# Four graph-attention layers on one core: normed rows turned by DMA instead of TensorE, and pieces of layer 0 moved from VectorE to ScalarE and GpSimd

## The chip, the cores and the metric

The kernel runs on one core of a Trainium2 chip. The core has TensorE (PE, matrix products, with a weight load of its own, PEld), VectorE (DVE), ScalarE (ACT), GpSimd (POOL), a queue engine (SP) that mostly starts transfers, and 16 DMA engines. The metric is the device time of one execution in microseconds (us); smaller is better. The kernel before takes 3050.61 us, the median of three runs between 3050.41 and 3050.61.

## The reference

x holds 16 graphs (batches) of 1024 nodes with 256 features, in float32; one adjacency matrix of 1024 x 1024 is shared by all. Four layers follow each other, each of the form

```
h = max(layernorm(x), 0)
x = x + attention_layer(h, adj)
```

- Layers 0 and 3 are graph attention with 4 heads of 64 features: Wh = h W; the score of the pair (i, j) is leaky_relu(s_i + t_j) with s and t from two vectors; softmax over the neighbours j; a weighted sum of Wh; ELU.
- Layer 1 is the same with one head of 256 features.
- Layer 2 takes its scores from a product of two projections, leaky_relu((h W1)(h W2)^T), masks and normalizes them in the same way, multiplies h W3, and ends in a ReLU.

All 16 batches are independent of each other; within one batch each layer needs the one before, and each needs all 1024 rows of x.

## The kernel before, in words

The kernel is written out for all 16 batches and 4 layers by `fast` (a second path, `general`, is there for inputs with extreme values and isn't entered here). A batch's x is one tile of 128 partitions x 8 row tiles x 256 features; 5 such tiles are held at a time, so several batches are at different layers at once.

**The order.** `Plan` is a planner in the kernel's source. Every piece of work is a step with an engine, a cost in us, a due time, the steps it must follow, and the buffers that it takes and gives. `Plan.order` plays this forward, on each engine always the due step whose inputs and buffers are there, and the instructions are then emitted in that order. So the order on each engine is fixed when the kernel is built, and each engine works through its own list. `PERIOD`, `START`, `LEAD`, `STEP`, `WHEN`, `LATER` and `AHEAD` set the due times: batch b starts layer l at about (b + START[l]) periods. A transfer is planned by `landed` as 256 KB in about 0.8 us and then 2.2 us until it is seen.

**One layer of one batch.** `Layer.prologue` takes mean and variance (L813, L814: on DVE), gets 1/sqrt on POOL (L849) and a shift on DVE (L852). Then, for four pairs of row tiles:

1. ACT norms two row tiles into `h` (L886, two instructions of 128x256).
2. TensorE turns them, so that features lie on partitions (`turned`, `turn`, L585). It treats a float32 value as two 16-bit halves, and turns each half with a 16-bit identity: 16 matmuls of 64x128 for a pair. This keeps every bit.
3. ACT joins the halves again from PSUM into `hTp` or `hT` (`kept`, L918, 128x1024 of 16 bits).
4. TensorE multiplies with the weights (`projected`, L572). ACT takes exponentials of the score columns (L949, L952), and the values are scaled by one of them: with one head on ACT (L954), with four heads on DVE (`scaled`, L960).

The score rows go to DRAM and come back spread over all partitions (`er_d`, `row`: L1028, L1041 on SP). In layers 0 and 3 (`steps_a`) DVE then builds one weight tile p of 128x512 per head, half and key tile (`weigh`, L1089: the larger of row and key factor, times the mask), and TensorE multiplies it with the values into `acc` (`attend`). After 8 key tiles the sum is inverted (L1122) and divided: on DVE (L1133), or on ACT, four instructions (L1136), where `filling` holds, which is layer 0 of batches 0 to 2 and layer 3 of batches 14 and 15. `elu` makes the ELU on ACT and DVE (L1060, L1061, L1065) and adds it to x on DVE (L1066). Layers 1 and 2 (`steps_b`) build p for all 8 key tiles of a half (L1179 in layer 1; L1206, L1207, L1211, L1212 in layer 2) and then multiply a query tile at a time into `accb`.

The first prologue of the run and the last (`direct`) differ: their score rows are spread by TensorE (L1002) and not by DRAM.

The mask is made once: the adjacency is compared with 0, turned by TensorE, and kept as four tiles of 16-bit floats.

Buffers that matter here: 8 p tiles, 4 PSUM tiles `pp` for all short products, 2 `acc` and 2 `accb`, 4 `h`, 2 `hTp`, 3 rows for four heads.

Of the kernel before, what the change touches and what calls it, by code (L numbers as in the profile page):

```python
# [10 lines left out]
BF16 = mybir.dt.bfloat16  # L11
I32 = mybir.dt.int32
U16 = mybir.dt.uint16
AF = mybir.ActivationFunctionType
OP = mybir.AluOpType
# [4 lines left out]
P = 128  # L20
# [20 lines left out]

PERIOD, EARLY = 190.0, 0.76
START = {0: 0.0, 1: 1.12, 2: 2.28, 3: 3.57}
LEAD = {0: 0.55, 1: 0.69, 2: 0.43, 3: 1.98}
STEP = {0: 0.0278, 1: 0.0451, 2: 0.105, 3: 0.0624}
WHEN = {  # L50
    (1, "weights"): ((-0.2631, 0.0266), (-0.1849, 0.0202)),
    (1, "attended"): ((0.3063, 0.0435), (0.1514, 0.2476)),
    (2, "weights"): ((0.0671, 0.0134), (0.1481, 0.0064)),
    (2, "attended"): ((0.514, 0.0835), (0.5175, 0.0062)),
}

LATER = {
    (0, 1): -0.958, (0, 2): -0.007, (1, 0): 0.06, (1, 1): 0.8, (2, 0): -0.065, (2, 2): 0.245, (3, 0): -0.357,
    (13, 3): 0.24, (15, 2): 0.02,
}  # L60
AHEAD = {
    (0, 2): 0.54, (1, 0): 0.48, (1, 1): 0.26, (2, 0): 0.16, (3, 0): -0.1,
}
# [466 lines left out]
def fast(  # L530
# [22 lines left out]
    bufs = {  # L553
        "x": 5, "val4": 2, "val1": 2, "hq": 1, "row4": 3, "row1": 2, "h": 4, "hTp": 2, "p": 8, "p1": 18,
        "u": 2, "o": 1, "ex4": 1, "o1": 2, "ex1": 2, "pp": 4, "acc": 2, "accb": 2,
# [44 lines left out]

    mask = [[const.tile([P, HT, HALF], BF16, name=f"mask{i}{j}") for j in range(2)] for i in range(2)]
    rdens = const.tile([P, B, NT], F32, name="rdens")
# [15 lines left out]
    def load_x(b, due, after=()):  # L618

        res = []  # L620
        for k in range(2):

            def fn(k=k):
                if k == 0:
                    x_tiles[b] = buf("x", [P, NT, F], name="xt")
                its = slice(k * HT, (k + 1) * HT)
                nc.sync.dma_start(
                    out=x_tiles[b][:, its, :], in_=x[b].rearrange("(t p) f -> p t f", p=P)[:, its, :]
                )

            s = plan.add(SP, 0.5, due, fn, after, take=() if k else ("x",))
            after = (s,)
            res += [landed(s, due, 512)] * HT
        return res
# [184 lines left out]
    class Layer:  # L819
        def __init__(self, b, layer):  # L820
            self.b, self.layer = b, layer
            self.heads, self.gat = LAYERS[layer]
            self.closed = []

            self.filling = layer == 0 and b < 3 or layer == 3 and b >= B - 2

        def prologue(self, due, step, stats, direct=False):
# [10 lines left out]
            ready = []  # L838
            parts = (slice(0, HT), slice(HT, NT)) if direct else (slice(0, NT),)
            for n, its in enumerate(parts):  # L840

# [27 lines left out]

                at = due - 2 * (direct and n == 0)  # L870
                s = plan.add(DVE, 0.2, at, norm, (*stats[its], ready[-1] if n else None))
# [3 lines left out]
            copies, evicted = [], []  # L875
            turns = {}
            run = 2
            for t0 in range(0, NT, run):
                at = due + t0 // 2 * step
                pairs, norms = range(t0, t0 + run, 2), []  # L880
                for t1 in pairs:

                    def normed(t0=t1):
                        for t in (t0, t0 + 1):
                            h = T["h", t] = buf("h", [P, F])
                            nc.scalar.activation(  # L886
                                h,
                                x_tiles[b][:, t, :],
                                AF.Relu,
                                bias=T["shift"][:, t : t + 1],  # L890
                                scale=T["rstd"][:, t : t + 1],
                            )

                    take = () if norms else ("h",) * run
                    norms.append(plan.add(ACT, 1.2, at, normed, (ready[t1], *norms), take=take))

                def turned(pairs=pairs):
                    for t0 in pairs:
                        tp = T["tp", t0] = buf("pp", [P, 2, KC, 2 * P], BF16)
                        for k in range(2):  # L900
                            bits = halves(T["h", t0 + k])
                            for c in range(KC):
                                for side in range(2):
                                    turn(tp[:, side, c, k * P : (k + 1) * P], bits[:, side, c * P : (c + 1) * P])

                n = len(pairs)
                s = plan.add(PE, 0.47 * n, at, turned, norms, take=("pp",) * n, give=("h", "h") * n)
                turns.update(dict.fromkeys(pairs, s))
            for n, t0 in enumerate(range(0, NT, 2)):
                at, s = due + n * step, turns[t0]  # L910

                def kept(t0=t0):
                    if self.gat:
                        T["hT", t0] = buf("hTp", [P, KC, 2 * P])
                    else:
                        T["hT", t0] = self.hT[:, :, t0 * P : (t0 + 2) * P]
                    bits = T["hT", t0].bitcast(U16).rearrange("p c (q s) -> p c q s", s=2)
                    nc.scalar.copy(bits, T["tp", t0].bitcast(U16).rearrange("p s c q -> p c q s"))  # L918

                s = plan.add(ACT, 0.95, at, kept, (s,), take=("hTp",) if self.gat else (), give=("pp",))  # L920
                copies.append(s)
                for k in range(2):
# [17 lines left out]

                    def evict(t=t):
                        to = self.val[:, t, :, :d]
                        of = T["pv", t][:, :F].rearrange("p (h d) -> p h d", h=heads)
                        if not self.gat:
                            nc.scalar.copy(to, of)
                            return
                        a = self.val[:, t, :, d : d + 1]

                        nc.scalar.activation(  # L949
                            a, T["pv", t][:, F + heads : cols].unsqueeze(2), AF.Exp, scale=1.0 / (SLOPE - 1.0)  # L950
                        )
                        nc.scalar.activation(self.ke[:, :, t], T["pv", t][:, F:cols], AF.Exp)  # L952
                        if heads == 1:
                            nc.scalar.mul(to, of, a[:, 0, :])  # L954

# [5 lines left out]

                    many = heads > 1
                    cost = 0.4 if many or not self.gat else 0.8
                    s2 = plan.add(ACT, cost, at, evict, (s2,), give=() if many else ("pp",))
# [85 lines left out]
        def elu(self, T, key, its, due, after, sizes, cols, give):  # L1050

            tag = f"ex{sizes[0]}"
            first, last = cols[0] == 0, cols[1] == F
            xs = lambda: x_tiles[self.b][:, its[0] : its[1], cols[0] : cols[1]]

            def up():
                if first:
                    T["ex", key] = buf(tag, [P, its[1] - its[0], F])
                o, ex = T["o", key][:, :, cols[0] : cols[1]], T["ex", key][:, :, cols[0] : cols[1]]
                nc.scalar.activation(ex, o, AF.Exp)  # L1060
                nc.scalar.activation(ex, ex, AF.Relu, bias=1.0, scale=-1.0)  # L1061

            def down():
                o, ex = T["o", key][:, :, cols[0] : cols[1]], T["ex", key][:, :, cols[0] : cols[1]]
                nc.vector.scalar_tensor_tensor(o, ex, -1.0, o, op0=OP.mult, op1=OP.max)  # L1065
                nc.vector.tensor_add(xs(), xs(), o)  # L1066

            s = plan.add(ACT, sizes[1], due, up, after, take=(tag,) if first else ())
            s = plan.add(DVE, sizes[2], due, down, (s,), give=(tag, *give) if last else give)
            if last:  # L1070
                for t in range(its[0], its[1]):
                    self.finish(t, due, (s,))
            return s
# [4 lines left out]
    def steps_a(lay, due, span):  # L1078
# [4 lines left out]
        for i in range(n):  # L1083
# [43 lines left out]
            def divide(half=half, hd=hd, on_act=on_act):  # L1127
# [11 lines left out]
            s = plan.add(  # L1139
                *((ACT, 0.8) if on_act else (DVE, 0.44)), at - early[0], divide, (s,),  # L1140
                take=("o",) if hd == 0 else (), give=("acc",),
            )

            if ending:
# [218 lines left out]
    for start, b, layer in sorted(order):  # L1363
# [8 lines left out]
        else:  # L1372
            due, step = SOON, 0.1
            stats = [statistics(b, t, due - (3 if t < HT else 1), (loads[b][t],)) for t in range(NT)]
        lay.prologue(due, step, stats, direct=(b, layer) in ((0, 0), (B - 1, 3)))
# [70 lines left out]
```

## Time and profile before

| | us |
|---|---|
| median of 3 runs | 3050.61 |
| the profiled execution, its own time | 3051.08 |
| its span, first to last instruction | 3049.3 |
| TensorE busy | 3009.3 (99%) |
| DVE busy | 2719.1 (89%) |
| ACT busy | 1461.6 (48%) |
| POOL busy | 127.6 (4%) |
| one batch in the middle (954.99 to 1140.39) | 185.40 |

The profile is one execution, taken by the hardware profiler. A row of its groups reads: source line, engine, operation, output <- inputs, shapes, count | busy time of the group in us, mean ns of one | idle time of the engine just before, and what ended it. Busy time counts overlapping neighbours once, so busy over count is less than the mean. "Waits" name who waited for whom. The chain is the work that ended last, followed back to the start. Matmul ends are modelled, so a busy TensorE isn't one at its peak. Lines such as L572 and L585 are those of helpers that every product or turn goes through. Transfers are issued by SP in the order of its list; its waits are listed apart.

### The profile page before, as it was taken

The numbers are of one execution on the slowest core, as the hardware profiler recorded it, in microseconds if no ns is written. First come the engines' busy times: TensorE is split into PE (matmuls) and PEld (weight loads), VectorE is DVE, ScalarE is ACT, GpSimd is POOL, SyncE is SP. The second block draws the span as 40 slices with busy tenths as digits, with TensorE's granted clock in tenths as the row PEclk, the third lists the DMA queues.
The fourth block names the chain that finished last, engine by engine and source line by source line (L and its number), as shares of the span: only waits on it lengthen the run. The fifth ranks groups of instructions, "written<-read, shape, count | busy, mean of one in ns | idle before, by whom it ended". The sixth has DMA issues, their size and how long they took to land.

```text
span 3049.3 us, 115063 instructions
## 1 busy us (share of the span) xinstructions
PE 3009.3 (99%) x52018; PEld 2508.5 (82%) x52018; DVE 2719.1 (89%) x5551; ACT 1461.6 (48%) x3352; POOL 127.6 (4%) x115
## 2 busy tenths in 40 slices
PE   7999999999999999999999999999999999999998
PEld 6887978778797887978888797887978879786877
DVE  8999968989889898998989989898998989986788
ACT  5563556544544446344454543546344463444443
POOL 1000000000000000000000000000000000000000
PEclk9999999999999999999999999999999999999999
DMA  3110003111010111101111011110111101000110
GB/s 127 51 51 23 27 16 97 38 40 48 20 58 26 37 55 25 58 21 37 51 34 55 19 41 47 37 48 18 52 37 37 55 21 46 23 30 25 30 33 24
DMA packets 82161, 123.41 MB, mean 40 GB/s; under 512 B 6976, under 2 KB 42496, under 8 KB 81664
## 3 DMA queue, kind: packets, MB, share of 16 engines
q1 hardware_dynamic: 81248, 115.47, 12.6%
q8 instruction: 409, 6.70, 0.9%
q14 instruction: 88, 0.72, 0.1%
q10 hardware_dynamic: 416, 0.52, 0.1%
HBM read 98.63 MB, written 17.33 MB: 38 GB/s over the span
## 4 chain that ended last, share of the span: by engine, by line
PE 95%; DVE 4%; issue 0%; DMA 0%; ACT 0%; SPq 0%; DVEq 0%
PE pp L572 33%; PE acc L572 30%; PE accb L572 29%; PE pp L585 4%; DVE p L1089 2%; DVE bn L813 0%; DVE xt L1066 0%; DMA xt<-in_x_dram 0%; DVE o L1065 0%; DVE mv L814 0%; PE pp L1002 0%; PE tpm L585 0%; PE er L585 0%; DVE rden L1122 0%; DVE parts L1308 0%
## 5 line engine op out<-in xcount | busy, mean ns | idle before, releaser
L1089 DVE SCALAR_TENSOR_TENSOR p<-row,ke,mask 128x512 f32<-128x512 f32 x2048 | 1413.2, 744 | 57.9 <-PE acc L572 54.4
L572 PEld LDWEIGHTS acc<-val,p 128*64 128x64 f32 x32768 | 1078.5, 139 | 71.5 <-issue 37.0
L572 PE MATMUL acc<-val,p 128*64 128x65 f32 x32768 | 1087.9, 223 | 17.6 <-DVE p L1089 16.9
L572 PE MATMUL accb<-val,p 128*64 128x257 f32 x8192 | 929.2, 380 | 0.4 <-issue 0.4
L572 PEld LDWEIGHTS accb<-val,p 128*64 128x64 f32 x8192 | 766.6, 136 | 103.2 <-issue 7.0
L572 PE MATMUL pp<-qT,hT 128*64 128x512 f32 x2048 | 457.6, 592 | 0.0
L572 PE MATMUL pp<-w,hTp 128*64 128x264 f32 (+1 forms) x3072 | 378.8, 386 | 0.0
L572 PEld LDWEIGHTS pp<-qT,hT 128*64 128x64 f32 x2048 | 189.1, 137 | 206.5 <-issue 204.3
L572 PEld LDWEIGHTS pp<-w,hTp 128*64 128x64 f32 x3072 | 267.6, 137 | 53.9 <-issue 7.7
L1246 ACT ACTIVATE o<-accb,rdens 128x256 f32<-128x256 f32 x128 | 60.6, 474 | 471.1 <-DVE rdens L1238 433.0
L886 ACT ACTIVATE h<-xt,nshift,rstd 128x256 f32<-128x256 f32 x512 | 273.1, 596 | 12.9 <-DVE nshift L852 12.9
L1211 DVE SCALAR_TENSOR_TENSOR p<-u,p 128x512 f32<-128x512 f32 x256 | 175.8, 687 | 62.1 <-ACT p L1207 61.5
L1206 ACT ACTIVATE u<-pp 128x512 f32<-128x512 f32 x256 | 152.7, 596 | 152.6 <-PE pp L572 137.3
L813 DVE BATCH_NORM_STATS2 bn<-xt 128x6 f32<-128x256 f32 x512 | 212.4, 415 | 14.8 <-DMA xt<-in_x_dram 5.2
L1244 ACT ACTIVATE o<-accb,rden 128x256 f32<-128x256 f32 x128 | 60.4, 472 | 337.9 <-DVE rden L1238 337.9
L918 ACT COPY hTp<-pp 128x1024 uint16<-128x1024 uint16 x192 | 190.4, 1011 | 58.2 <-PE pp L585 56.9
L849 POOL TENSOR_TENSOR rstd<-rstd,neg_half 128x8 f32<-128x8 f32 (+1 forms) x66 | 117.9, 1786 | 2108.0 <-DVE rstd L846 1643.8
L1212 DVE TENSOR_TENSOR p<-p,mask 128x512 f32<-128x512 f32 x256 | 177.2, 692 | 8.8
L1179 DVE SCALAR_TENSOR_TENSOR p<-row,ke,mask 128x512 f32<-128x512 f32 x256 | 183.6, 741 | 0.0
L1207 ACT ACTIVATE p<-pp,shift_col 128x512 f32<-128x512 f32 x256 | 174.8, 683 | 0.0
L585 PEld LDWEIGHTS <-h 128*64 128x64 bf16 x4096 | 149.4, 111 | 21.3 <-issue 13.4
L1060 ACT ACTIVATE ex<-o 128x1024 f32<-128x1024 f32 (+1 forms) x195 | 122.1, 626 | 90.6 <-DVE o L1133 86.3
(84 smaller groups left out, 1910.9 us busy)
## 6 DMA issues: line engine op xcount, KB each, us to landing
row<-er_d SPq DMA_DIRECT2D x272, 256.0 KB
xt<-in_x_dram SPq DMA_DIRECT2D x32, 512.0 KB
out_dram<-xt SPq DMA_DIRECT2D x31, 512.0 KB
raw<-in_adj_dram SPq DMA_DIRECT2D x4, 1024.0 KB
raw<-in_adj_dram SPq DMA_DIRECT2D x16, 256.0 KB
w<-in_L_gnn_W_dram SPq DMA_DIRECT2D x2, 256.0 KB
wraw<-in_L_gnn_W_dram SPq DMA_DIRECT2D x2, 256.0 KB
er_d<-er_s SPq DMA_DIRECT2D x30, 16.0 KB
```

Source lines behind the costliest of these rows:

```text
L572: nc.tensor.matmul(to[c : c + COLS], stationary[:, c : c + COLS], moving, start=start, stop=stop, skip_group_check=True,)
L585: nc.tensor.transpose(to[c : c + COLS], of[:, c : c + COLS], ident_b)
L813: nc.vector.bn_stats(st, x_tiles[b][:, t, :])
L886: nc.scalar.activation(h, x_tiles[b][:, t, :], AF.Relu, bias=T["shift"][:, t : t + 1], scale=T["rstd"][:, t : t + 1],)
L918: nc.scalar.copy(bits, T["tp", t0].bitcast(U16).rearrange("p s c q -> p c q s"))
L1060: nc.scalar.activation(ex, o, AF.Exp)
L1089: nc.vector.scalar_tensor_tensor(p, lay.rows[half, hd], lay.ke[:, lay.heads + hd, jt : jt + 1], mask_of(half, jt), op0=OP.max, op1=OP.mult)
L1179: nc.vector.scalar_tensor_tensor(p, lay.rows[half, 0], lay.ke[:, 1, jt : jt + 1], mask_of(half, jt), op0=OP.max, op1=OP.mult)
L1206: nc.scalar.activation(u, e, AF.Exp, scale=1.0 - SLOPE)
L1207: nc.scalar.activation(p, e, AF.Exp, bias=shift_col, scale=SLOPE)
L1211: nc.vector.scalar_tensor_tensor(p, u, 1.0, p, op0=OP.max, op1=OP.mult)
L1212: nc.vector.tensor_mul(p, p, mask_of(half, jt))
```

## The change

The turning of normed rows leaves TensorE in 62 of 64 prologues. ACT splits each normed pair into planes of 16-bit halves (`split`), SP starts a DMA that transposes 8 blocks of 128x128 (`move`), and ACT joins the halves from the landed tile (`kept`). The two `direct` prologues turn float32 whole on TensorE, 4 transposes a pair, and copy. `filling` now holds for layer 0 of every batch, and where it holds (and the prologue isn't direct) ACT also scales the values, four instructions a tile, in place of DVE; ACT divides in all of layer 0; and POOL adds the ELU to x. The mask is 8-bit; with two tiles `planes` and two `turned` more, the on-chip memory it gives up is used. The first batch's x comes in three parts (2, 2 and 4 row tiles) rather than two. All due times are set anew. The product lists carry 4096 fewer 16-bit transposes of h and 32 float32 ones more; SP carries 248 transposing transfers more, POOL 35 additions.

```diff
+PARTS = (((0, 4), (4, 8)), ((0, 2), (2, 4), (4, 8)))
-PERIOD, EARLY = 190.0, 0.76
-START = {0: 0.0, 1: 1.12, 2: 2.28, 3: 3.57}
-LEAD = {0: 0.55, 1: 0.69, 2: 0.43, 3: 1.98}
-STEP = {0: 0.0278, 1: 0.0451, 2: 0.105, 3: 0.0624}
+PERIOD, EARLY = 190.0, 0.74
+START = {0: 0.0, 1: 0.96, 2: 2.3, 3: 3.63}
+LEAD = {0: 0.7841, 1: 0.4991, 2: 0.193, 3: 1.8815}
+STEP = {0: 0.028, 1: 0.0997, 2: 0.0747, 3: 0.0167}
...
-        "x": 5, "val4": 2, "val1": 2, "hq": 1, "row4": 3, "row1": 2, "h": 4, "hTp": 2, "p": 8, "p1": 18,
+        "x": 5, "val4": 2, "val1": 2, "hq": 1, "row4": 3, "row1": 2, "h": 4, "planes": 2, "turned": 2, "hTp": 2, "p": 8, "p1": 18,
...
-    mask = [[const.tile([P, HT, HALF], BF16, name=f"mask{i}{j}") for j in range(2)] for i in range(2)]
+    mask = [[const.tile([P, HT, HALF], U8, name=f"mask{i}{j}") for j in range(2)] for i in range(2)]
...
-        for k in range(2):
+        for t0, t1 in PARTS[b == 0]:
...
-            self.filling = layer == 0 and b < 3 or layer == 3 and b >= B - 2
+            self.filling = layer == 0 or layer == 3 and b >= B - 2
...
-                def turned(pairs=pairs):
-                    for t0 in pairs:
-                        tp = T["tp", t0] = buf("pp", [P, 2, KC, 2 * P], BF16)
-                        for k in range(2):
-                            bits = halves(T["h", t0 + k])
-                            for c in range(KC):
-                                for side in range(2):
-                                    turn(tp[:, side, c, k * P : (k + 1) * P], bits[:, side, c * P : (c + 1) * P])
...
+                def turned(t0=t0):
+                    tp = T["tp", t0] = buf("pp", [P, KC, 2 * P])
+                    for k in range(2):
+                        for c in range(KC):
+                            nc.tensor.transpose(
+                                tp[:, c, k * P : (k + 1) * P], T["h", t0 + k][:, c * P : (c + 1) * P], ident
                             )
...
+                def split(t0=t0):
+                    to = T["planes", t0] = buf("planes", [P, 2, KC, 2, P], U16)
+                    for k in range(2):
+                        of = T["h", t0 + k].bitcast(U16).rearrange("p (c n s) -> p s c n", c=KC, s=2)
+                        nc.scalar.copy(to[:, :, :, k, :], of)
+
+                def move(t0=t0):
+                    tp = T["tp", t0] = buf("turned", [P, 2, KC, 2 * P], U16)
+                    nc.sync.dma_start_transpose(
+                        out=tp.rearrange("p s c (k n) -> p (s c k) n", k=2),
+                        in_=T["planes", t0].rearrange("p s c k n -> p (s c k n)"),
+                    )
...
+                    if direct:
+                        nc.scalar.copy(T["hT", t0], T["tp", t0])
+                        return
                     bits = T["hT", t0].bitcast(U16).rearrange("p c (q s) -> p c q s", s=2)
-                    nc.scalar.copy(bits, T["tp", t0].bitcast(U16).rearrange("p s c q -> p c q s"))
-
-                s = plan.add(ACT, 0.95, at, kept, (s,), take=("hTp",) if self.gat else (), give=("pp",))
+                    nc.scalar.copy(bits, T["tp", t0].rearrange("p s c q -> p c q s"))
+
+                take = ("hTp",) if self.gat else ()
+                if direct:
+                    s = plan.add(PE, 0.47, at, turned, (s,), take=("pp",), give=("h", "h"), wide=True)
+                    s = plan.add(ACT, 0.6, at, kept, (s,), take=take, give=("pp",))
+                else:
+                    s = plan.add(ACT, 1.25, at, split, (s,), take=("planes",), give=("h", "h"))
+                    s = plan.add(SP, 0.5, at, move, (s,), take=("turned",))
+                    s = landed(s, at, 256, give=("planes",))
+                    s = plan.add(ACT, 1.02, at, kept, (s,), take=take, give=("turned",))
...
-                        if heads == 1:
-                            nc.scalar.mul(to, of, a[:, 0, :])
+                        for hd in range(0 if many else heads):
+                            nc.scalar.mul(to[:, hd, :], of[:, hd, :], a[:, hd, :])
...
-                    many = heads > 1
-                    cost = 0.4 if many or not self.gat else 0.8
+                    many = heads > 1 and (direct or not self.filling)
+                    cost = 0.4 if many or not self.gat else 0.8 if heads == 1 else 1.15
...
-                nc.vector.tensor_add(xs(), xs(), o)
-
+                if not on_pool:
+                    nc.vector.tensor_add(xs(), xs(), o)
+
+            on_pool = self.filling and first and last
...
+            if on_pool:
+                s = plan.add(POOL, 2.7, due, lambda: nc.gpsimd.tensor_add(xs(), xs(), T["o", key]), (s,), give=gives)
...
-                *((ACT, 0.8) if on_act else (DVE, 0.44)), at - early[0], divide, (s,),
+                *((ACT, 0.8) if on_act else (DVE, 0.44)), at - early[0], divide, (s, T.get(("divided", half))),
```

`WHEN`, `LATER` and `AHEAD`, tables of due times like those shown, are set anew as well and left out here.

## The prediction

> **What bounds the kernel now.** I read the page from the top: engines first, then the chain that ended last, then stretches of time, then the rows of what is edited.
>
> ```profile
> PE 3009.3 (99%) x52018; PEld 2508.5 (82%) x52018; DVE 2719.1 (89%) x5551; ACT 1461.6 (48%) x3352; POOL 127.6 (4%) x115
> ...
> PE pp L572 33%; PE acc L572 30%; PE accb L572 29%; PE pp L585 4%; DVE p L1089 2%; DVE bn L813 0%; DVE xt L1066 0%; DMA xt<-in_x_dram 0%; DVE o L1065 0%; DVE mv L814 0%; PE pp L1002 0%; PE tpm L585 0%; PE er L585 0%; DVE rden L1122 0%; DVE parts L1308 0%
> ```
>
> TensorE is idle for 40 us of 3049.3, and the chain stands on it for 95%. The stretches say where that idle time lies: the first 100 us, one batch's period in the middle, the end.
>
> ```profile
> 0.00:100.00 100.00, 75.70 (x1586) 63.62 (x1586) 84.81 (x190) 50.02 (x157) 11.23 (x20) 0.97 0.33 108
> 954.99:1140.39 185.40, 185.40 (x3242) 156.96 (x3239) 169.63 (x346) 86.70 (x191) 7.42 (x6) 1.00 0.13 39
> 2980.00:3049.30 69.30, 55.84 (x1360) 48.97 (x1354) 60.69 (x106) 23.65 (x70) 0.00 (x0) 0.93 0.08 26
> ```
>
> Columns: stretch, then busy time of PE, weight load, DVE, ACT and POOL, clock, DMA share, GB/s. In the middle TensorE never stops; DVE is 91% busy and ACT 47%. So work taken from TensorE counts in full there, until DVE (15.8 us free per period) or a wait takes over. The rows and one spot of two timelines (DVE, POOL) that carry the prices:
>
> ```profile
> L585 PE MATMUL pp<-ident_b,h 128*64 128x128 bf16 x4096 | 162.9, 220 | 0.0
> L886 ACT ACTIVATE h<-xt,nshift,rstd 128x256 f32<-128x256 f32 x512 | 273.1, 596 | 12.9 <-DVE nshift L852 12.9
> L1061 ACT ACTIVATE ex<-ex 128x1024 f32<-128x1024 f32 x63 | 66.8, 1060 | 2.0
> L960 DVE TENSOR_TENSOR val<-pp,val 128x256 f32<-128x256 f32 x256 | 102.0, 417 | 16.7 <-ACT ke L952 16.3
> L1133 DVE TENSOR_TENSOR o<-acc,rden 128x256 f32<-128x256 f32 x217 | 92.1, 424 | 6.8
> L1066 DVE TENSOR_TENSOR xt<-xt,o 128x1024 f32<-128x1024 f32 x63 | 77.2, 1225 | 2.2
> L1136 ACT ACTIVATE o<-acc,rden 128x64 f32<-128x64 f32 x156 | 36.1, 316 | 58.7 <-DVE rden L1122 51.2 <-DVE both L1347 3.6 <-DVE xt L1066 3.4
> ...
> 62.85 4.73 DVE L1089 SCALAR_TENSOR_TENSOR p<-row,ke,mask 128x512 f32<-128x512 f32 x6 [0.49 <-PE acc L572]
> ...
> 61.15 3.24 POOL L675 TENSOR_TENSOR wa<-w,a_bc 128x256 f32<-128x256 f32 x4 [19.14 <-DVE a_bc L665]
> ...
> SPq L1041 <- DVE p L1089: 1725.0, 200, 42.2
> ```
>
> Busy over count is what one instruction adds, since neighbours overlap: 0.53 us for L886, 0.23 for L1136.
>
> **What the Trainium skill says.** "DMA: Bandwidth & Descriptors", Latency and other measured facts, gives a DMA transpose 261 GB/s; no transposing DMA is in this trace. "VectorE: DVE Perf Modes", The three transpose paths, gives 1309 ns for one 128x128 16-bit block by DMA: that is my upper price. "SBUF — State Buffer", Who interferes with whom: a DVE instruction with two SBUF inputs and a GpSimd instruction that reads SBUF exclude each other for the whole instruction. The timeline lines agree: elsewhere a run of seven L1089 takes 4.73 us; at 62.85 us, beside the POOL multiplies, six take that long, so one step of 0.67 us was lost. "VectorE: DVE Perf Modes", What auto-detection actually checks: the fast two-input mode needs every tensor to be 16-bit. L1089 reads a float32 row either way, so an 8-bit mask should not move its mode; no run here shows an 8-bit input.
>
> **The change part by part**, summed against the profiled span of 3049.3 us (its run took 3051.08; the median is 3050.61, 1.3 us above the span).
>
> *Turning leaves TensorE.* 62 of 64 prologues lose 4 groups of 16 matmuls: 248 groups. The chain's exact share for these matmuls is 3.6% of 3049.3, or 110 us over 256 groups: 0.43 us each. 248 x 0.43 = **-107 us**. The two direct prologues keep 8 groups, now of 4 float32 transposes; L1002 (the same kind, 64 in 9.9 us) makes that 0.62 each, +1.5 us. **-105 us**.
>
> *ACT takes it up.* 496 split copies of 512 elements, read from SBUF. Between L1061 at 256 (0.42) and at 1024 elements (1.06) I interpolate 0.63: +312 us. The 248 joins read SBUF instead of PSUM: 1.06 (L1061) against 0.99 (L918, 190.4 over 192): +17. The divisions of 104 more heads (13 batches' layer 0) are 416 instructions, 96 us; the scaling of 128 tiles (120 in layer 0, 8 in layer 3 of batch 14) is 512, 118 us. ACT goes from 1462 to about 2005 us, 67%. It does not become the bound by its sum.
>
> *DVE gets lighter.* -128 x 0.40 (L960), -104 x 0.42 (L1133), -35 x 1.225 (L1066) = -51 - 44 - 43 = -138 us, to 2581. None of it is on the chain in the middle; it is worth nothing directly.
>
> *POOL gets 35 additions* of 128x1024. From L675's four of 256 columns in 2.79 us (61.15's four needed 3.24 beside DVE), one costs about 2.6 to 2.9 us, and by the lock above DVE's next weighting waits as long. Lower bound 0 (the next DVE instructions read PSUM), upper 35 x 2.8 = 98 us of DVE. I take 2.6 each, 91 us: DVE 2672. TensorE is covered by the p ring of 8 tiles: half full, it holds 4 x 0.48 us of matmuls, 1.9 us. 35 x (2.6 - 1.9) = **+25 us**. What is late next behind the addition itself is the closing statistics of layer 0; layer 1 is due long after.
>
> *8-bit mask.* 2560 DVE instructions read it. 687 ns (L1211, float32 second input) against 692 (L1212, bf16) shows no effect of width: I take 0, bounds 0 and +0.07 us each (179 us of DVE).
>
> *The new wait.* A join on ACT now waits for split, SP's issue, transfer and landing. Everything behind it on ACT waits too: evictions that free PSUM, the exponentials, the divisions that free acc and accb; and TensorE waits for those. Price of the transfer: issue 0.32 us (the row of DMA issues on SP), 256 KB at 261 GB/s = 1.0 us (estimate from the skill), and a landing of about 2.3 us: after a small er_d store SP goes on to the row load behind it 1.8 us later (2398.58 to 2400.39 in SP's timeline), and its longest wait on such a store is 2.9 us. Sum about 3.6 us. Upper bound: 8 blocks x 1.309 + 0.3 = 10.8. I take 3.6, as one transfer of 8 blocks should not pay its fixed part eight times. Cover: I added up, in the built order, the ACT work that stands between each split and its join. Median 5.1 us; 25 of 248 have under 3.5, 68 under 4.5, 147 under 5.5. The shortfall over all pairs is 57 us at 3.6 us, 198 at 5.5, 368 at 6.5, 1212 at 10.8. ACT has a third of its time free and TensorE has work queued from other layers, so I let a third through: **+19 us**.
>
> *The fill.* In the first 100 us nothing covers a longer prologue. The turn was 0.43 + 0.99 us; now it is 1.26 + 3.6 + 1.06: 4.5 us more for the first pair. Three prologues stand in that stretch (layer 0 of batches 1 and 2, layer 1 of batch 0): **+13 us**. The finer loading of the first x and the shifted start times I cost at nothing: x's load waits are 5.2 us in all, and the order in the middle is as dense as before.
>
> *SP* gets 248 more issues, 79 us of time in a queue that mostly sleeps. 108 of them stand right behind a row or weight load, and row loads already wait 1725 us for L1089 to free a row. A transpose behind such a load is late when DVE is late; I put nothing on it, and carry it as a rival. DMA grows by 65 MB on 123 MB at a 14% share.
>
> Sum: -105 + 25 + 19 + 13 = -48: span 3001, median **3003 us**; by the roughness of the three give-backs, 2975 to 3030.
>
> **Rivals.** *All of it arrives* (2950, say 2944 to 2975): POOL finds gaps and transfers land inside 3 us. For it: 4 x 0.66 us of L1089 run on undisturbed beside the small POOL powers. Against: the lost step at 62.85. *The landing is late* (slower): between 5 and 6 us from split to data, ACT stops at most pairs. A third of the shortfall plus the other give-backs eats the gain at about 5.7 us; at 7 us the shortfall is 462, and a third to a half gives 3085 to 3170. For it: the price per block in the skill, and that transposes share a queue with loads; against: the 14% share. *SP's order*: loads held for rows hold transposes, with the same look and the size of a late landing, 3040 to 3100. *DVE becomes the bound*: mask conversion of 0.07 us with the lock makes DVE 2850, 95% of any span; with the gaps it has now (11%) that is 3050 to 3150. *The cut is inert*, DVE setting the pace at today's period: within 0.2%.
>
> **Chances.** Forecast 0.48, all arrives 0.17, late landing 0.20, SP's order 0.05, DVE bound 0.07, inert 0.03. A measurement of this kernel can tell about 0.2% (6 us) from no change. Faster: 0.48 + 0.17 and a little of SP's order = 0.66; same 0.05; slower 0.29. The range starts under the full gain's middle (2950) and ends in the late landing's upper half (3130), leaving some 0.05 below and 0.13 above.
>
> **What would show it.** Right: a period near 181 us in the middle with TensorE over 97% busy, no h matmuls, joins waiting little for DMA, DVE runs stretched by up to 2.6 us where POOL adds. Wrong: TensorE waits on ACT evictions and ACT's joins wait hundreds of us for DMA (landing late), L1089 over 0.75 us (mask), or SP's transposes waiting on DVE. What I know least is the transposing transfer's time.

## The result, and the profile after

The changed kernel takes 3024.74 us (median of four runs, 3023.33 to 3027.57), the kernel before 3050.51 beside it (3050.02 to 3050.61). The ratio is 0.9917, with an interval of 0.9900 to 0.9934: 26 us faster. The forecast was 3003, its own range 2975 to 3030.

Two lines of the page of the changed kernel: busy time by engine, and the chain of work that ended last.

```profile
PE 2929.2 (97%) x47954; PEld 2248.8 (74%) x47954; DVE 2632.4 (87%) x5286; ACT 1926.1 (64%) x4776; POOL 225.7 (7%) x151
...
PE pp L575 30%; PE accb L575 26%; PE acc L575 26%; DVE p L1109 8%; DVE bn L815 2%; DVE o L1080 1%; DVE mv L816 1%; DVE xt L1082 1%; DVE p L1200 1%; ACT o L1156 0%; DMA xt<-in_x_dram 0%; ACT hTp L925 0%; DVE p L1233 0%; ACT ex L1076 0%; ACT ex L1075 0%
```

TensorE lost 80 us of busy time and its idle time grew from 40 to 94 us. The chain, which stood on TensorE for 95% and on DVE for 4% before, now stands on TensorE for 82% and on DVE for 14%. The same columns by stretch (stretch, PE, weight load, DVE, ACT, POOL, clock, DMA share, GB/s):

```profile
0.00:100.00 100.00, 76.78 (x1474) 60.30 (x1474) 81.89 (x177) 59.39 (x197) 15.90 (x23) 0.97 0.38 117
100.00:200.00 100.00, 83.89 (x1428) 67.72 (x1428) 88.86 (x195) 65.86 (x184) 15.90 (x9) 0.88 0.28 64
1388.00:1570.10 182.10, 179.03 (x2984) 138.28 (x2982) 162.05 (x328) 117.28 (x287) 13.07 (x8) 1.00 0.27 63
2950.00:3023.00 73.00, 57.67 (x1316) 49.39 (x1312) 61.21 (x111) 25.06 (x78) 6.20 (x3) 0.93 0.08 25
```

A batch in the middle takes 182.1 us where it took 185.4, and TensorE stands for 3.1 us of it where it stood for none. The rows that answer to the ones priced:

```profile
L1109 DVE SCALAR_TENSOR_TENSOR p<-row,ke,mask 128x512 f32<-128x512 f32 x2048 | 1450.8, 762 | 69.6 <-PE acc L575 63.0 <-ACT mask L743 2.6 <-ACT row L1021 1.5
L907 ACT COPY planes<-h 128x512 uint16<-128x512 uint16 x496 | 280.8, 617 | 0.4 <-DMA turned<-planes 0.4
L925 ACT COPY hTp<-turned 128x1024 uint16<-128x1024 uint16 x184 | 212.2, 1169 | 21.0 <-DMA turned<-planes 21.0
L1156 ACT ACTIVATE o<-acc,rden 128x64 f32<-128x64 f32 x572 | 132.8, 321 | 107.2 <-DVE rden L1142 92.0 <-POOL xt L1089 12.9 <-DVE nshift L854 1.9
L1089 POOL TENSOR_TENSOR xt<-xt,o 128x1024 f32<-128x1024 f32 x35 | 91.1, 2603 | 1047.7 <-DVE o L1080 1038.5 <-DVE rden L1259 9.2
L925 ACT COPY hT<-turned 128x1024 uint16<-128x1024 uint16 x64 | 74.2, 1161 | 13.0 <-DMA turned<-planes 13.0
```

A split takes ACT 0.62 us (0.63 forecast) and adds 0.57 to its busy time, since neighbours overlap; a join adds 1.15 (1.06), an addition on POOL 2.60 (2.6). The joins waited for their transfers for 34 us in all, 27 times. The weighting on DVE, 1413 us before, takes 38 us more. One place on POOL's timeline and on DVE's shows why:

```profile
1493.49 2.81 POOL L1089 TENSOR_TENSOR xt<-xt,o 128x1024 f32<-128x1024 f32 x1 [7.86 <-DVE o L1080]
...
1493.33 3.52 DVE L1109 SCALAR_TENSOR_TENSOR p<-row,ke,mask 128x512 f32<-128x512 f32 x2
1496.77 0.15 DVE L1259 RECIPROCAL rden<-accb 128x1 f32<-128x1 f32 x1
1496.85 0.73 DVE L1109 SCALAR_TENSOR_TENSOR p<-row,ke,mask 128x512 f32<-128x512 f32 x1
```

Two weightings, 1.4 us elsewhere, take 3.52 us: the second lasts 2.85 us and ends 0.55 us after POOL's addition. Over the whole run 25 DVE instructions, each beside another of the 35 additions, last over 2 us; all 25 read two tiles. Beside the other ten additions no DVE instruction is stretched in this way. The waits of TensorE in the changed kernel (us in all, times, longest):

```profile
PE acc L575 <- DVE p L1109: 45.0, 40, 4.3
PE pp L899 <- ACT h L884: 11.8, 1, 11.8
PE acc L575 <- ACT o L1156: 9.1, 11, 1.2
PE pp L575 <- ACT hTp L925: 5.4, 5, 2.4
PE pp L575 <- ACT hT L925: 4.7, 5, 1.9
```

The first was 16.9 us before. Only the last two have to do with the new transfers, 10 us together.

### The profile page after: what moved, and what is told of

It is laid out like the page before. It is cut to its first block, busy times and chain, and to the rows that moved or that the text cites. A ratio compares the mean times of both kernels' runs of the same rounds, so it can differ in the third digit from the quotient of the medians.

```text
span 3023.1 us, 108612 instructions
## 1 busy us (share of the span) xinstructions
PE 2929.2 (97%) x47954; PEld 2248.8 (74%) x47954; DVE 2632.4 (87%) x5286; ACT 1926.1 (64%) x4776; POOL 225.7 (7%) x151
## 4 chain that ended last, share of the span: by engine, by line
PE 82%; DVE 14%; ACT 2%; issue 1%; DMA 0%; SPq 0%; DVEq 0%; ACTq 0%
PE pp L575 30%; PE accb L575 26%; PE acc L575 26%; DVE p L1109 8%; DVE bn L815 2%; DVE o L1080 1%; DVE mv L816 1%; DVE xt L1082 1%; DVE p L1200 1%; ACT o L1156 0%; DMA xt<-in_x_dram 0%; ACT hTp L925 0%; DVE p L1233 0%; ACT ex L1076 0%; ACT ex L1075 0%
## 5 line engine op out<-in xcount | busy, mean ns | idle before, releaser
L1109 DVE SCALAR_TENSOR_TENSOR p<-row,ke,mask 128x512 f32<-128x512 f32 x2048 | 1450.8, 762 | 69.6 <-PE acc L575 63.0
L575 PEld LDWEIGHTS accb<-val,p 128*64 128x64 f32 x8192 | 700.2, 137 | 159.3 <-issue 3.9
L575 PEld LDWEIGHTS pp<-qT,hT 128*64 128x64 f32 x2048 | 149.6, 137 | 237.7 <-issue 230.9
L575 PEld LDWEIGHTS pp<-w,hTp 128*64 128x64 f32 x3072 | 240.6, 139 | 93.2 <-issue 11.4
L907 ACT COPY planes<-h 128x512 uint16<-128x512 uint16 x496 | 280.8, 617 | 0.4 <-DMA turned<-planes 0.4
L851 POOL TENSOR_TENSOR rstd<-rstd,neg_half 128x8 f32<-128x8 f32 (+2 forms) x67 | 124.0, 1850 | 1711.7 <-DVE rstd L848 1077.6
L925 ACT COPY hTp<-turned 128x1024 uint16<-128x1024 uint16 x184 | 212.2, 1169 | 21.0 <-DMA turned<-planes 21.0
L1156 ACT ACTIVATE o<-acc,rden 128x64 f32<-128x64 f32 x572 | 132.8, 321 | 107.2 <-DVE rden L1142 92.0
L1200 DVE SCALAR_TENSOR_TENSOR p<-row,ke,mask 128x512 f32<-128x512 f32 x256 | 179.9, 741 | 0.0
L969 ACT ACTIVATE val<-pp,val 128x64 f32<-128x64 f32 (+1 forms) x640 | 179.5, 347 | 0.0
```

What stands on the lines that cost most here:

```text
L575: nc.tensor.matmul(to[c : c + COLS], stationary[:, c : c + COLS], moving, start=start, stop=stop, skip_group_check=True,)
L907: nc.scalar.copy(to[:, :, :, k, :], of)
L925: nc.scalar.copy(bits, T["tp", t0].rearrange("p s c q -> p c q s"))
L969: nc.scalar.mul(to[:, hd, :], of[:, hd, :], a[:, hd, :])
L1109: nc.vector.scalar_tensor_tensor(p, lay.rows[half, hd], lay.ke[:, lay.heads + hd, jt : jt + 1], mask_of(half, jt), op0=OP.max, op1=OP.mult)
L1200: nc.vector.scalar_tensor_tensor(p, lay.rows[half, 0], lay.ke[:, 1, jt : jt + 1], mask_of(half, jt), op0=OP.max, op1=OP.mult)
```

## The experiments

Theory at the outset: the matmuls leave for -105 us and POOL's additions give 25 back; the other 53 us come from late transfers and a longer fill. Rivals: DVE or ACT takes over as the bound; the new due times make a worse order. The first four runs test the terms one by one.

**Additions on DVE**, issued at the same place of the order.

```
-lambda: nc.gpsimd.tensor_add(xs(), xs(), T["o", key])
+lambda: nc.vector.tensor_add(xs(), xs(), T["o", key])
```

> The changed kernel with its 35 additions of x issued on DVE at the same place in the order, POOL idle there. Changed kernel: 3024.7 us. If POOL's addition only moved the cost (DVE stood about 48 us beside POOL by the trace, and its own additions cost 35 x 1.14 = 40 us), the time stays within 6 us: 3018 to 3030. If the additions on POOL were a real relief for DVE, it is 15 to 40 us slower: 3040 to 3065.

Measured: 3006.57 us (3005.6 to 3007.01), 18 us under the changed kernel, though DVE has 43 us more to do. The weighting's row is back where it was:

```profile
L1109 DVE SCALAR_TENSOR_TENSOR p<-row,ke,mask 128x512 f32<-128x512 f32 x2048 | 1412.8, 742 | 69.5 <-PE acc L575 62.6 <-DMA row<-er_d 3.0 <-ACT row L1021 1.5
```

No DVE instruction lasts over 2 us here, and TensorE waits 34.5 us for p where it waited 45.0. This agrees with the exclusion that the Trainium skill states ("SBUF — State Buffer", Who interferes with whom). A second path, later freed buffers because POOL adds more slowly than DVE, is not tested apart: ACT's division waited 12.9 us for POOL's addition, and waits 8.9 us for DVE's here.

**No additions**: the step stays in the order and issues nothing.

```
-lambda: nc.gpsimd.tensor_add(xs(), xs(), T["o", key])
+lambda: None
```

> The changed kernel with those 35 additions left out (layer 0's result is not added to x, so the output differs). It takes POOL's hold on DVE away and puts nothing in its place. Theory that the hold costs TensorE what I priced (25 us): 3000, between 2990 and 3008. Rival, that the p ring hides it and the order of the work loses the time: 3018 to 3025.

Measured: 2998.42 (2995.01 to 3000.13). POOL's additions cost 26 us against none at all, DVE's 8.

**No transfers**: the join reads a tile of zeros that lies ready.

```
-tp = T["tp", t0] = buf("turned", ...)
-nc.sync.dma_start_transpose(out=tp..., in_=T["planes", t0]...)
+T["tp", t0] = nil
```

> The changed kernel with the 248 transposing transfers left out; ACT still splits, and joins from a tile of zeros at the same place without waiting (the output differs). Theory that late landings let through 19 us, and the longer prologue 13 us more in the fill: 2992 to 3006. Rival, that the transfers are covered nearly everywhere and ACT's added work or DVE costs the time: 3018 to 3025.

Measured: 3022.5 (3020.64 to 3023.19), 2 us under the changed kernel, less than the executions of one kernel differ among themselves. The transfers are hidden; late landing is out as a cause, at the start and end as well (the table below).

**The mask alone**: the kernel before with the 8-bit mask.

```
-const.tile([P, HT, HALF], BF16, name=f"mask{i}{j}")
+const.tile([P, HT, HALF], U8, name=f"mask{i}{j}")
```

> The kernel before with nothing changed but the mask's type, 8-bit for 16-bit. Theory: DVE reads it at the same pace, 3050.6 within 4 us. Rival, a conversion cost of up to 0.07 us on 2560 DVE instructions: 3060 to 3150, and L1089 at 0.75 to 0.81 us where it was 0.744.

Measured: 3049.85, ratio 1.0000 (0.9991 to 1.0009); L1089 there takes 743 ns, as before. The mask costs nothing.

The matmuls forecast at -105 and the additions measured at +26 give 3050 - 105 + 26 = 2971. Against 3024.7 some 53 us were still to be explained, and neither the transfers nor the mask explains them. The next four ask whether TensorE's time counts in full, or DVE's or ACT's load takes its place.

**The kernel before without the h matmuls**, in its own order.

```
+if not direct:
+    T["tp", t0] = nil
+    continue
 tp = T["tp", t0] = buf("pp", [P, 2, KC, 2 * P], BF16)
```

> The kernel before in its own order and with the 8-bit mask; the 248 groups of h matmuls of the 62 prologues that are not direct are left out, and the join reads a tile of zeros on-chip instead. So TensorE loses 107 us and nothing else changes. Of the 53 us that the changed kernel lacks against 3050 - 105 + 26 = 2971: if TensorE's time counts in full and they are lost to ACT's added work or to the new order, this gives 2943 (2935 to 2952). If DVE sets the pace as soon as TensorE is shorter, this order, with DVE at 2719 us, gains clearly less: 2970 to 3005, with TensorE waiting on L1089's p for 50 us or more.

Measured: 2982.29 (2981.86 to 2983.2), ratio 0.9782. Only 68 us come. The time lies in the second range, but its sign is missing: TensorE waits 23 us for p in the whole run, not 50. Its middle, and TensorE's waits in it:

```profile
900.00:2250.00 1350.00, 1338.73 (x21993) 991.55 (x21990) 1257.23 (x2576) 658.24 (x1424) 59.87 (x46) 1.00 0.13 39
...
PE acc L573 <- DVE p L1095: 4.5, 7, 0.6
PE pp L573 <- ACT hTp L924: 3.5, 7, 0.5
PE pp L573 <- DVE val L966: 2.2, 7, 0.3
```

TensorE, never idle there before, now stands about once a batch each for DVE's weights, ACT's joins and DVE's scaling, and DVE, the next in load, is 93% busy. That could be an order laid out around a piece of work that is gone; the run with the turning alone, below, bears on it.

**TensorE time put back** into the changed kernel: the first of two products of each projection is issued twice.

```
-for c in range(KC):
+for c in range(KC) if direct else (0, *range(KC)):
```

> The changed kernel in its own order, with the first of the two products of every projection (496 of them, all but the direct prologues') issued twice, the second overwriting the first: 496 x 2 matmuls of 264 columns at 0.124 us = 123 us of TensorE put back beside the place it was taken from. If TensorE's time counts in full in this order too: 3024.7 + 123 = 3148. If TensorE now waits for DVE or ACT in most periods (94 us idle in all, some 3 us a period), that idle time takes up to 45 us of it: 3100 to 3125. Under 3100: TensorE no longer sets the pace.

Measured: 3223.01 (3222.86 to 3223.18). The expected addition was too small: the trace has four matmul records for each product where I had counted two, and TensorE's busy time rose by 211 us (2929.2 to 3140.4). The span rose by 198. So TensorE's time counts for 94% in this order too; the idle time took up 13 us.

**Scaling and division back on DVE**, with the additions, at the places where ACT had them.

```
-for hd in range(0 if many else heads):
-    nc.scalar.mul(to[:, hd, :], of[:, hd, :], a[:, hd, :])
+if heads == 1:
+    nc.scalar.mul(to[:, 0, :], of[:, 0, :], a[:, 0, :])
+elif not many:
+    nc.vector.tensor_mul(to, of, a.to_broadcast([P, heads, d]))
...
-if not on_act:
+if not on_act or lay.layer == 0 and lay.b > 2:
```

> The 35 additions on DVE (as in the run that gave 3006.6), and layer 0's scaling (128 tiles) and the divisions of batches 3 to 15 on DVE as well, at the places where ACT had them; the rest of the change stays. DVE gets 51 + 44 = 95 us more, ACT 214 us less. My prediction held DVE's relief to be worth nothing directly: 3000 to 3010, or less if ACT's load was what made TensorE wait. If DVE's bursts set the pace at the places where TensorE stands, 3006.6 + 30 to 95: 3035 to 3100.

Measured: 3024.44 (3020.32 to 3024.73), 18 us over the run with only the additions on DVE. DVE's relief is worth something in this order, less than the lower end of the second expectation and more than the first allowed.

**No split and no transfers** in the changed kernel.

```
 def split(t0=t0):
-    to = T["planes", t0] = buf("planes", ...)
-    for k in range(2): ... nc.scalar.copy(to[:, :, :, k, :], of)
+    return
```

> The changed kernel with the 496 split copies left out, and the transfers too; the join reads zeros. ACT loses 281 us against the run without transfers (3022.5), DVE and TensorE nothing. If ACT's added work holds the evictions and the divisions up, this gives 2985 to 3005. If the loss lies with DVE, or in the order of the work, it stays at 3015 to 3023; the fill (first product into accb at 153 us) shows separately whether the prologues' length counts there: 3 x 1.2 us at most.

Measured: 3018.94 (3018.54 to 3019.86), 3.6 us under the run without transfers. ACT's 281 us of splitting are hidden.

What is left is the order. The next three make it anew from the old due times; the last doubles the h matmuls in the order before.

**The turning alone**: the kernel before, its due times, scaling, divisions and additions, with split, transfer and join of the changed kernel (and the 8-bit mask for room; a division also waits for the one before it, as in the changed kernel).

```
-s = plan.add(PE, 0.47 * n, at, turned, norms, take=("pp",) * n, give=("h", "h") * n)
-s = plan.add(ACT, 0.95, at, kept, (s,), take=..., give=("pp",))
+s = plan.add(ACT, 1.25, at, split, (s,), take=("planes",), give=("h", "h"))
+s = plan.add(SP, 0.5, at, move, (s,), take=("turned",))
+s = landed(s, at, 256, give=("planes",))
+s = plan.add(ACT, 1.02, at, kept, (s,), take=take, give=("turned",))
```

> The kernel before with nothing but the turning changed (and the mask in 8 bits, for room): split on ACT, transposing transfer, join, in 62 prologues; direct prologues turn float32. Due times, x loading, scaling, division and additions as before; the order is made anew by the planner. The run without h matmuls gave 2982.3 in the old order; the transfers cost 2 us and the split 4 us in the changed kernel's order. If the turning is as cheap here as there, and the rest of the change (additions on POOL, new due times) is what gives the time back: 2983 to 3000. If the turning itself gives it back where the order was not set for it: 3010 to 3050.

Measured: **2979.57** (2978.85 to 2980.86), ratio 0.9773 (0.9756 to 0.9789), 45 us faster than the whole change and the fastest of all runs here. Its middle, and its row of DMA issues on the page (median from issue to landing at the end, us):

```profile
900.00:2250.00 1350.00, 1348.17 (x22396) 1104.37 (x22393) 1276.00 (x2611) 791.95 (x1690) 58.82 (x46) 1.00 0.28 64
...
turned<-planes SPq DMA_TRANSPOSE x248, 3.2
```

TensorE is idle for 1.8 us of these 1350 (11.3 without the h matmuls in the old order), though DVE is busier still, 95%. So DVE's load alone was not what held TensorE there.

**The old due times** in the changed kernel: the seven tables of the kernel before, `PERIOD` to `AHEAD`.

```
-START = {0: 0.0, 1: 0.96, 2: 2.3, 3: 3.63}
+START = {0: 0.0, 1: 1.12, 2: 2.28, 3: 3.57}
...
```

> The changed kernel with the due-time tables of the kernel before, the order made anew from them; all else as changed. If the new due times are what makes the start 19 to 23 us longer (first product into accb at 154.7 us, against 131.6 in the old order without h matmuls): first such product at 132 to 142, total 3000 to 3013. If the start is longer because of scaling on ACT and additions on POOL: total 3020 to 3040, first such product still at 150 or later. An order not set for the change can also be worse by itself: over 3040, idle time in the middle.

Measured: 3014.95 (3013.4 to 3015.74), 10 us faster than with the new ones. The first product into accb stands at 151.4 us (154.7), so the gain isn't at the start, where I had put it.

**The old due times and the additions on DVE**, both edits.

> As the run before, and the 35 additions back on DVE. The additions cost 18 us in the order of the changed kernel; the same 12 to 22 us are to be seen here, so 12 to 22 us under the run with the old due times alone. Equal to it would mean that the cost of the additions lies in the order that they stand in.

Measured: 2985.00 (2983.77 to 2986.59). The additions cost 30 us in this order, more than the 12 to 22 expected; with them on POOL, 32 DVE instructions last over 2 us in this order, where 25 did. Against the run that differs from it in the due times alone (3006.57), the new tables cost 21.6 us. The middle of four kernels, in this order: before, changed, changed with the additions on DVE, and that with the old due times as well.

```profile
900.00:2250.00 1350.00, 1350.00 (x23717) 1136.51 (x23713) 1235.91 (x2502) 623.80 (x1382) 51.97 (x42) 1.00 0.14 40
```

```profile
900.00:2250.00 1350.00, 1329.19 (x22064) 1027.77 (x22062) 1209.22 (x2432) 873.20 (x2131) 97.30 (x60) 1.00 0.29 64
```

```profile
900.00:2250.00 1350.00, 1332.94 (x22206) 1061.29 (x22204) 1210.44 (x2449) 877.82 (x2139) 55.77 (x43) 1.00 0.27 63
```

```profile
900.00:2250.00 1350.00, 1349.74 (x22469) 1053.80 (x22465) 1228.30 (x2491) 893.75 (x2177) 54.22 (x46) 1.00 0.29 64
```

The first number after the length is TensorE's busy time. With the old tables TensorE is idle for 0.3 us of 1350; with the new ones for 17, and for 21 with the additions on POOL. Where the 17 us go, in the waits of the third of these kernels over the same stretch:

```profile
PE acc L575 <- ACT o L1156: 7.4, 8, 1.2
PE acc L575 <- DVE p L1109: 5.4, 6, 1.0
PE acc L575 <- DVE rden L1142: 1.9, 5, 0.4
PE pp L575 <- ACT hT L925: 1.9, 1, 1.9
```

Once a batch, TensorE waits for a division to free acc, and about once for a weight tile.

**The h matmuls twice** in the kernel before.

```
-for k in range(2):
+for k in range(2) if direct else (0, 1, 0, 1):
     bits = halves(T["h", t0 + k])
```

> The kernel before in its own order, with the h matmuls of the 248 groups of the 62 prologues issued twice over the same PSUM tile. TensorE is idle for 0.8 us between its first and its last product into accb there, so all that is added counts. My prediction priced a group at 0.43 us (the chain's share of 110 us over 256 groups): +107, 3157. The run without these matmuls lowered TensorE's busy time by 91 us, which is 0.367 us a group: +91, 3141. The first would mean that leaving them out lost 16 us elsewhere; the second that the price was too high by 16 us.

Measured: 3157.71 (3157.01 to 3158.36), ratio 1.0354: +108 us. A group costs 0.435 us, as priced. Leaving the groups out brought 68 and adding them costs 108: the price was right. Of the missing 40 us, 22 are time in which TensorE stands when the work is gone (40 us idle before, 62 without); its busy time fell by only 91 us, so the other 17 or so lie in longer records of the matmuls that stayed. Why those are longer was not tested.

**The runs in one account.** From the trace, each span is cut at the start of the multiplies into accb that end the first and the third quarter of the 8192: between lie eight batches of the middle, the rest is start and end. The numbers of the other large matmuls in that middle are the same in every kernel here. Each row is one profiled execution.

| kernel (us) | middle, 8 batches | start and end | span |
|---|---|---|---|
| before | 1483.3 | 1566.0 | 3049.3 |
| before, h matmuls twice | 1540.5 | 1615.8 | 3156.2 |
| before, no h matmuls | 1450.4 | 1529.5 | 2979.9 |
| turning alone | 1428.9 | 1549.3 | 2978.3 |
| changed, old due times, additions on DVE | 1429.8 | 1552.1 | 2981.9 |
| changed, old due times | 1445.1 | 1566.4 | 3011.5 |
| changed, additions on DVE | 1448.7 | 1556.6 | 3005.2 |
| changed | 1454.1 | 1569.0 | 3023.1 |
| changed, no transfers | 1453.6 | 1567.7 | 3021.3 |
| changed, no transfers, no split | 1453.6 | 1564.5 | 3018.1 |

Eight batches hold 128 groups, 128 x 0.435 = 56 us. The turning alone gains 54.4 in the middle, nearly all of it. Without h matmuls but in the old order it is 33. As the split and the transfer only add work, the new order is what is left to bring the other 21. At the start and end it is the other way round: 16.7 against 36.5, so the two kernels take nearly the same time in all (2979.6 and 2982.3).

## Why the prediction was right and wrong

The direction, the bound and the price of the turning were right; the forecast time was 22 us too low. From before to changed, by the spans of neighbouring rows of the table: turning alone -71.0; scaling and division on ACT and the finer loading of the first x +3.6; new due times +23.3; additions on POOL +17.9. The sum is -26.2, the spans differ by 26.2. The last two depend on which goes first: with the additions first they cost 29.6 and the due times 11.6, together 41 either way. The medians give 5, 22 and 18 for the last three steps.

The three terms that belong to the turning (-105, +19 and +13) add up to -73, and the turning alone measures -71. That agreement is luck: by the runs the first was about 14 too large, the second was 2 and the third is open, and the errors cancel.

*Turning leaves TensorE, -105.* The price holds: 0.43 forecast, 0.435 measured. "Counts in full" holds in the middle where the order is made anew from tables that suit it (-54.4 of 56). It fails at the start and end: there the same removal gives 36.5 us (1566.0 to 1529.5), where the remaining 120 groups are worth 52. TensorE's idle time there grows by 9 us (40.0 to 49.2), and its other matmuls have longer records. That is about 14 us too much in this term.

*POOL's additions, +25.* The size was right: +18 in the changed kernel against DVE, +26 against none, and +30 against DVE with the old due times. What it was made of was not: all 35 were to hold DVE, 91 us in all; 25 do, and DVE's busy time is 50 us above that without additions (2632.4 against 2582.8). So TensorE loses 18 to 26 of 50 us where 25 of 91 was forecast: the p tiles cover less than supposed, and part of the agreement is luck. Of the 18, 12 fall at the start and end.

*Late landing, +19.* Wrong. The latency was right (3.6 forecast, 3.2 measured from issue to landing), and joins did wait, but for 34 us where the shortfall was put at 57, and ACT had the time: taking the transfers away brings 2 us. "A third through" was a guess with no row behind it, and the rival built on it falls with it.

*The fill, +13.* Too high in the changed kernel: taking out transfer and split, which was to be nearly the whole of the longer prologue, shortens start and end by only 4.5 us. The turning alone has 19.8 us more at the start and end than the kernel without h matmuls, but the orders of these two differ, and no run separates the longer prologue from the order there. This stays open.

*Due times and loading of x, 0.* This is the step that failed: "the order in the middle is as dense as before". No line of a profile stood behind it, and the planned order shows in which sequence instructions stand, not whether each finds its input. The new tables cost 23 us with the additions on DVE, 19 of them in the middle, and 12 with the additions on POOL, 9 of them in the middle. TensorE stands there for freed acc buffers and for weight tiles, which no cost of an instruction shows. I had put those waits under late landing.

*DVE's relief, 0.* Not quite: put back at ACT's places it costs 18 us in the changed order. With the old due times, having it on ACT is no gain: 2985.0 against 2979.6 with all of it on DVE, and the finer x loading is in that difference too. *Mask, 0*: right. *SP*: each transposing issue held it for 1.23 us, not 0.32; as the transfers cost 2 us in all, this doesn't show in the time.

Of the rivals, "all of it arrives" came nearest to what the turning by itself can do, but even that took 2979.6, above its middle of 2950. Of the signs named for a right forecast, TensorE over 97% busy in the middle (98.5), the stretched DVE instructions and the short waits of the joins are there, and the period is 181.8 us on the mean of eight batches where one near 181 was forecast: nearly the right period by luck, since late landing stood where the due times belong.

## What to carry to other kernels

In a kernel whose order is fixed beforehand, a removed piece of work may be worth less than its time until the order around it is made anew: here 33 us of 56 in the middle, then 54. Leave it out in the old order first, then double it; the difference (here 108 against 68) is what a new order may still bring, and here it brought this in the middle but not at the start and end. When a change comes with a new set of tuned times, run it once with the old ones: a retuned order is an edit with a price of its own. Moving an addition off a busy DVE to POOL was no relief here, 18 to 30 us slower, because DVE's instructions beside it mostly read two tiles.

## What the runs showed of the hardware

- A transposing transfer of 256 KB, SBUF to SBUF, eight 16-bit blocks of 128x128, lands 3.2 us after issue (median of 248, the turning alone), as fast as a plain row load of 256 KB on the same page (3.2). It holds SP for 1.23 us where a plain transfer holds it for 0.32. The prediction's estimate with the rate in the Trainium skill ("DMA: Bandwidth & Descriptors", Latency and other measured facts) came to 3.6 us in all. That is near, but its part for the issue was 0.32, so the rate itself is not confirmed. Eight times the price of one block (10.5 us) is not what is seen.
- Beside an addition of 128x1024 on POOL, DVE instructions of 0.4 to 1.2 us that read two tiles last up to 2.88 us (25 cases in the changed kernel, 32 with the old due times, none with the additions on DVE).
- TensorE's granted clock in the stretch from 100 to 120 us was 0.83 before, with TensorE busy for 18.57 us, and 0.68 in the changed kernel, with 11.71. In the first 20 us it was 1.00 in both, with TensorE busy for 6. So idle time alone doesn't set it; what does was not tested.
- DVE takes 684 ns to write a 128x512 mask tile in 8 bits, 414 ns in 16 bits; reading it in 8 bits costs the weighting nothing (743 ns with the mask alone, 744 before).
